# A graph layer on one core: edges sorted tile by tile into three places a bin, instead of three tiles together into nine

## The chip, the cores and the metric

The kernel runs on one core of one Trainium2 chip. The metric is the device time of one execution in microseconds (us), the median of several runs. Of the engines, TensorE (PE) multiplies matrices, VectorE (DVE) and ScalarE (ACT) work elementwise, GpSimd (POOL) issues the indirect transfers here, and SyncE (SP) issues most of the plain ones. All transfers share the core's 16 DMA engines. Matmuls write into PSUM, a small memory of banks with 2 KB per partition; everything else lies in SBUF (128 partitions) or in DRAM.

## The reference

A graph has 6250 nodes with 64 features and 206250 directed edges with 64 features. Each edge takes the features of one of its nodes (`col`), makes a 128-wide hidden vector, and adds its result to its other node (`row`):

```python
msg = concatenate([x[col], edge_attr], axis=1)       # 128 wide
h = relu(msg @ W1a.T + b1a)                          # 128 wide, per edge
h = h @ W1b.T + b1b
sums = segment_sum(h, row, num_segments=n_nodes)
agg = sums / maximum(counts, 1.0)[:, None]
z = relu(concatenate([x, agg], axis=1) @ W2a.T + b2a) @ W2b.T + b2b
out = concatenate([z, x], axis=1) @ Wr.T + br
y = layernorm(x + out)
```

The edges come sorted by `dst`, which is the node whose features are gathered; the node that receives the sum (`src`) is in no order. Bringing each edge's hidden vector to the node that it is added to is what most of the kernel does. The second matrix of the edge network is linear, so the kernel applies it after the sum, per node.

## The kernel before

**Tiles, blocks, bins.** The edges are padded to 1612 tiles of 128, grouped in 124 blocks of 13 tiles. The receiving nodes are grouped in 49 bins of 128. An edge's row is 130 numbers (`W`): its 128 hidden values, a one for the count, and the number of its node inside its bin. The goal is to have, for each bin, tiles of 128 rows that all belong to the bin; then a one-hot matrix of the node numbers (`nodes_of`, L1504, on DVE) and one matmul per tile (`summed`, L1524) add them to the bin's 128 sums. Matmuls in plain f32 run as two instructions each; the profile counts these.

**Two ways for a row.** Tiles of a block go one of two ways.

- *Direct*: the first layer is computed per tile (`hidden`, matmul L1372, ReLU L1376 on ACT into the ring `orow` of 4 blocks), and GpSimd scatters the 128 rows of the tile with one indirect transfer (`scatter`, L1396) to rows of DRAM (`rows`) that belong to their bins. The place of an edge in its bin is its rank, counted over all blocks by a running count on DVE (`carried`, `bins_of`, the scan L1065) and two bf16 matmuls (`counts_of`, L1104 and L1105); `slots` turns it into the row number `rowidx`.
- *Joined* (blocks 4 to 109, six of the 13 tiles, as two joins of three): the inputs of the edges, not their rows, are sorted on TensorE. A join has 441 fixed places (49 bins of nine, `SLOTS`) and 64 spare places. `join_ranks` and `join_places` give each of the join's 384 edges the next of the nine places of its bin; those that come too late go to the spare places, numbered by `join_past` and `join_at_slots`. `marks` makes a one-hot matrix of 128 x 512 for each tile: two of three on DVE (L1222), the third on ACT in two steps (L1227, L1228). `join` multiplies edge features (`side` and, for the low part, `rest`) with the marks; the three tiles add up in one PSUM bank, with a one-pass f32 type and 512 columns (L1256). ACT copies the result to `rj`. `join_rows`, one step later, computes the first layer from `rj` in chunks of 126 or 128 columns (L1273, L1280, L1281), and `join_store` writes the fixed places with SP to `fixed` in DRAM. Since each join has the same places, no indirect transfer is needed for these. The spare places (`overs`) are scattered by GpSimd as one tile, four blocks later, together with that block's direct tiles.

Empty places are rows of zeros, which cost a sum like others: they make tiles for the matmuls of L1524.

**Epochs.** Rows in DRAM can be summed only when they have landed. The scatters are cut in three epochs of 110, 12 and 2 blocks, each with its own `rows`; inside an epoch, the first tiles of a bin can be read as soon as so many blocks are done that they must be full (`FULL`). The rows in `fixed` can be read in stages of three tiles of places each. A plan worked out when the kernel is built (`groups_at`, with `RATES` as the most tiles per step) gives each step its groups of sums; `read` loads them with SP into nine buffers `rt`, `collect` adds the results to `part`.

**Order.** The loop `for k, ep_ in enumerate(epoch_of)` makes one step per block. PE, ACT, DVE and SP work in the order in which the step issues their instructions: counts of block k+1, first layer of block k (in two or four parts), `join_rows` of block k-1, first half of a group of sums, ranks of block k+1, the last part of the first layer, `join` of block k, second half of the sums. The scatters of block k are issued two steps later (`LEAD`). Some wait by hand for progress of the PE in step k+1 (`pace`, `PACED`), so that scatters don't overtake the first layer and leave it without a lead. Blocks 0 to 3 and 110 to 123 have no joined tiles. During the first steps the kernel also loads `x` (`load_x`, L857), makes tables of the nodes' part of the first layer (`y_rows`, L903) and windows of them (`window`, L1342), and clears the DRAM rows (`clear`).

After the last scatter the last epoch is summed, and 17 groups of nodes go through mean, node network and layer norm (`Nodes`, from L1914).

Of the kernel before, what the change touches and what calls it, by code (L numbers as in the profile page):

```python
# [9 lines left out]
F32 = mybir.dt.float32  # L10
# [443 lines left out]
EPOCHS = (110, 12, 2)  # L454
# [3 lines left out]
FULL = ((3, 6, 9, 12), (1,), ())  # L458
# [5 lines left out]
PRE, AHEAD_FROM, EVERY = 9, 10, 2  # L464
RATES = {0: 55, 2: 18, 3: 10}
RING = 8
# [5 lines left out]
JOIN, JOINS, MARKS = 3, 2, 3  # L472
JOIN_FROM, JOIN_TO = 4, 110
SLOTS, PARTS, WHOLE = 9, 3, 42
RUN = SLOTS // PARTS
SPARE = 64
OVER = 4
OVERS = 7
SORTED = 512
PACED = range(PRE, 123)  # L480
SIDES, ENATS, CHUNK = 2, 2, 2
ON_ACT = 1
# [11 lines left out]
def fast_path(  # L494
# [69 lines left out]
    def joined(k):  # L564
        if not JOIN_FROM <= k < JOIN_TO:
            return 0
        return JOINS
# [4 lines left out]
    def over(k):  # L572

        return int(k >= OVER and joined(k - OVER) > 0)
# [4 lines left out]
    def past_slots(nodes):  # L579

        mean = JOIN * P * nodes * (1 / N - 1 / E)
# [13 lines left out]
    def edges_of(b, n, first=0):  # L595
# [4 lines left out]
        joins = sum(joined(k - OVER) for k in blks if over(k))  # L600
# [3 lines left out]
        return nodes, mean + joins * more, SPREAD * (mean + joins * spread) ** 0.5  # L604
# [50 lines left out]
    GROUPS = -(-NJOIN * PARTS // P)  # L655
    for i in range(GROUPS):
        at = next(k for k in range(JOIN_TO + 1) if join_at[k] * PARTS >= min(P * (i + 1), NJOIN * PARTS))
        hi_ = by_bin((i + 1) * RUN, (i + 1) * RUN)
# [5 lines left out]
    PADT = 4  # L664
# [3 lines left out]
    for e, ep_ in enumerate(epochs):  # L668
        ep_.trash = P * sum(over(k) for k in range(ep_.first, ep_.end))
        ep_.rows = dram.tile([ep_.trash + NB * ep_.stride, W], F32, name=f"rows{e}")  # L670
    ALL = -(-GROUPS * P // (PARTS * JOINS)) * JOINS
    fixed.rows = [dram.tile([ALL * n, W], F32, name=f"fixed{n}") for n in (MAIN, MID)]
# [38 lines left out]
    mvs = const.tile([P, MV, W + 1], F32, name="mv")  # L711
# [33 lines left out]
    def bins(c0, c1):  # L745
# [4 lines left out]
        nc.vector.tensor_copy(hi[:, blks, :BLK], of)  # L750
# [5 lines left out]
    nc.vector.tensor_copy(mvs[:, :, H:], ident[:, None, WIDE : WIDE + 3].to_broadcast([P, MV, 3]))  # L756
    nc.vector.tensor_tensor(mvs[:, :, W], mvs[:, :, W], mvs[:, :, H], op=ALU.add)
# [6 lines left out]
    with (  # L764
# [32 lines left out]
        sorts = [op.tile([P, JOINS * RUN + 1, W], F32, name=f"sorted{i}") for i in range(2)]  # L797
        overs = [op.tile([P, W + 1], F32, name=f"over{i}") for i in range(OVERS)]

# [15 lines left out]
        def join_top():  # L815
            t = Top("join")
            t.marks = [t.tile([P, JOIN, SORTED], F32R, f"marks{i}") for i in range(MARKS)]
            t.sides = [t.tile([P, JT, P], F32R, f"side{i}") for i in range(SIDES)]
            t.rests = [t.tile([P, JT, D], F32R, f"rest{i}") for i in range(SIDES)]
            t.enats = [t.tile([P, JT, D], F32, f"enat{i}") for i in range(ENATS)]  # L820
            t.rjs = [t.tile([P, JOINS * (FIXED + SPARE)], F32, f"rj{i}") for i in range(2)]
# [3 lines left out]
            for side in t.sides:  # L825
                nc.gpsimd.memset(side[:, :, WIDE].bitcast(F32), 1.0)
                nc.gpsimd.memset(side[:, :, WIDE + 1 :].bitcast(F32), 0.0)
            return t
# [106 lines left out]
        def starts_at(tiles):  # L935
# [11 lines left out]
        one_w = const.tile([P, P], BF16, name="one_w")  # L947
        nc.vector.memset(one_w, 1.0)
# [13 lines left out]
        z_ps, near_f, bins_w = (  # L962
            steady[:, RAMP + 2 + HALF * T + a :][:, :n] for a, n in ((0, JT), (JT, NEAR), (JT + NEAR, HALF))
        )
        assert RAMP + 2 + HALF * T + JT + NEAR + HALF <= BANK
        NQB = 2 * HALF
        assert NB == NQB - 1
        bin_ramp = bins_w.bitcast(BF16)
        bins_b = lent(2 * NT + NG * P * 3 // 2 + NEAR * WIN + 3 * P + P // 2, HALF)
        nc.vector.tensor_copy(bins_b.bitcast(BF16), ramp_b[:, :NQB])  # L970
        nc.vector.memset(bins_b.bitcast(BF16)[:, NB:], -1.0)
        nc.vector.tensor_copy(bins_w, bins_b)
# [8 lines left out]

        codes = [const.tile([P, SORTED], F32, name=f"codes{i}") for i in range(JOINS)]

        def join_consts():


            for i, c in enumerate(codes):
                mid, main, past_ = c[:, :MID], c[:, MID : FIXED], c[:, FIXED : FIXED + SPARE]
                if i > 0:
                    past_, main, mid = c[:, :SPARE], c[:, SPARE : SPARE + MAIN], c[:, SPARE + MAIN : FIXED + SPARE]  # L990
                nc.vector.memset(c[:, FIXED + SPARE :], -1.0)
                main = main.rearrange("p (r a b) -> p a r b", a=PARTS, r=RUN)
# [1103 lines left out]
```

## Time and profile before

| What | Before |
|---|---|
| median of 3 runs | 1470.9 us (1469.45 to 1473.61) |
| profiled execution | 1471.28 us |
| its span, first to last instruction | 1469.1 us |
| mean granted TensorE clock | 0.972 |
| busy: PE, DVE, ACT, POOL | 1360.7, 1258.5, 1068.0, 1079.8 us |
| DMA | 380.88 MB, mean 259 GB/s |
| scatters (L1396) | 976 direct, 106 late |
| sum matmuls (L1524) | 3962, two a tile |

The page's slices are 40 equal parts of the span, about 36.7 us each; a digit is the busy share in tenths. In a group's row, the number behind x counts instructions, then come busy us and the mean ns of one; behind the second bar stands the idle time of the engine ahead of these instructions, with what ended it. In a timeline a row is: start, duration, engine, line, operation, and in brackets the idle time before it and its releaser. The duration of a matmul holds its way through the array, so that matmuls overlap; their cost in a row of many is read from start to start. "issue" names idle time in which the profile shows nothing that the engine waited for.

### The profile page before, as it was taken

How to read it: one execution, taken by the hardware profiler on the slowest of the kernel's cores; microseconds unless marked ns; L12 is line 12 of the kernel's file. 1: busy time of each engine (PE TensorE's matmuls, PEld its weight loads, DVE VectorE, ACT ScalarE, POOL GpSimd, SP SyncE). 2: the span in 40 equal slices, each digit the busy share in tenths (PEclk: the TensorE clock that was granted, in tenths of full speed). 3: DMA queues.
4: the chain of work that ended last, by engine and by line, in shares of the span. 5: the costliest groups of instructions: out<-in, count | busy, mean ns of one | idle time of the engine just before them, and what ended most of it. 6: DMA issues, size and time to landing. Idle time of an engine off the chain costs nothing.

```text
span 1469.1 us, 32367 instructions
## 1 busy us (share of the span) xinstructions
PE 1360.7 (93%) x10258; PEld 1201.3 (82%) x10258; DVE 1258.5 (86%) x2704; ACT 1068.0 (73%) x2309; POOL 1079.8 (74%) x1163
## 2 busy tenths in 40 slices
PE   5688888879999999999999999999999989999796
PEld 5566666668888888888889888888888889998685
DVE  8588777788888988999999999999999788797686
ACT  3389988888888888888988989898888743331014
POOL 5777777777777777777777777777777777777733
PEclk9699999999999999999999999999999999999898
DMA  8878977899999999999998978888888899998773
GB/s 204 247 227 271 271 241 236 252 286 262 297 269 294 284 288 277 269 259 271 268 262 253 266 229 247 244 252 251 234 255 257 260 307 336 294 314 257 246 237 95
DMA packets 264910, 380.88 MB, mean 259 GB/s; under 512 B 45418, under 2 KB 202146, under 8 KB 264730
## 3 DMA queue, kind: packets, MB, share of 16 engines
q1 hardware_dynamic: 196521, 270.41, 64.3%
q0 software_dynamic: 34624, 72.09, 15.4%
q10 hardware_dynamic: 33584, 36.22, 8.3%
q8 instruction: 84, 1.38, 0.4%
q14 instruction: 97, 0.79, 0.2%
HBM read 215.06 MB, written 163.48 MB: 258 GB/s over the span
## 4 chain that ended last, share of the span: by engine, by line
PE 65%; DMA 12%; ACT 7%; DVE 7%; issue 5%; POOL 3%; ACTq 1%; SPq 0%; DVEq 0%; POOLq 0%
PE h_ps L1524 26%; PE h_ps L1256 14%; PE h_ps L1372 10%; DMA rows<-orow,rowidx 10%; PE h_ps L1273 6%; POOL rows L1396 2%; ACT orow L1376 1%; PE cnt_ps L1104 1%; PE cnt_ps L1105 1%; PE h_ps L1281 1%; PE h_ps L1280 1%; DMA rows<-over,rowidx 1%; ACT rhs L1327 1%; DVE had L1065 1%; ACT rhs L1329 1%
## 5 line engine op out<-in xcount | busy, mean ns | idle before, releaser
L1396 POOL DMA_INDIRECT rows<-orow,rowidx x976 | 951.9, 975 | 308.1 <-issue 158.9
L1524 PE MATMUL h_ps<-rt,oh 128*128 128x129 f32 x3962 | 484.5, 277 | 14.3 <-DVE oh L1504 10.8
L1524 PEld LDWEIGHTS h_ps<-rt,oh 128*128 128x128 f32 x3962 | 470.6, 193 | 24.3 <-DVE oh L1504 13.7
L1504 DVE TENSOR_TENSOR oh<-ramp,rt 128x768 f32<-128x768 bf16 (+3 forms) x409 | 312.1, 797 | 42.1 <-DMA rt<-rows 31.5
L1372 PE MATMUL h_ps<-mv,rhs 124*128 124x128 f32 x1952 | 276.4, 286 | 28.9 <-ACT orow L1376 28.9
L1372 PEld LDWEIGHTS h_ps<-mv,rhs 124*128 124x128 f32 x1952 | 256.7, 198 | 42.8 <-ACT orow L1376 31.5
L1256 PE MATMUL h_ps<-marks,side 128*128 128x512 f32 x636 | 266.0, 428 | 8.8 <-ACT orow L1376 8.3
L1222 DVE TENSOR_TENSOR marks<-codes,ramp 128x1024 fp32r<-128x1024 f32 x212 | 253.5, 1214 | 0.0
L1256 PE MATMUL h_ps<-marks,rest 128*64 128x512 f32 x636 | 218.3, 397 | 0.0
L1376 ACT ACTIVATE orow<-h_ps 128x384 f32<-128x384 f32 (+1 forms) x284 | 150.7, 536 | 57.1 <-PE h_ps L1372 49.2
L1065 DVE TENSOR_TENSOR_SCAN had<-ramp,bins 128x450 bf16<-128x450 bf16 (+3 forms) x124 | 145.1, 1170 | 28.6 <-ACT bins L1086 13.6
L1273 PE MATMUL h_ps<-mv,rj 128*126 128x130 f32 x1272 | 160.7, 275 | 7.9 <-ACT rj L1261 7.9
L1256 PEld LDWEIGHTS h_ps<-marks,side 128*128 128x128 f32 x636 | 121.7, 191 | 52.9 <-ACT orow L1376 10.7
L1273 PEld LDWEIGHTS h_ps<-mv,rj 128*126 128x126 f32 x1272 | 149.6, 188 | 10.5 <-ACT rj L1261 10.2
L1228 ACT ACTIVATE marks<-marks,ones 128x512 fp32r<-128x512 f32 x212 | 153.1, 722 | 6.9
L1227 ACT ACTIVATE marks<-codes,z_act 128x512 fp32r<-128x512 f32 x212 | 155.3, 732 | 0.0
L1327 ACT ACTIVATE rhs<-rhs,from_win 60x896 f32<-60x896 bf16 (+1 forms) x116 | 129.5, 1117 | 2.8
L1329 ACT ACTIVATE rhs<-rhs,ones 60x896 f32<-60x896 f32 (+1 forms) x116 | 129.3, 1115 | 2.9
L1396 POOL DMA_INDIRECT rows<-over,rowidx x106 | 103.3, 974 | 32.3 <-issue 11.0
L1256 PEld LDWEIGHTS h_ps<-marks,rest 128*64 128x64 f32 x636 | 87.5, 138 | 31.6 <-ACT marks L1228 2.3
L1363 ACT CAST orow<-lohi 128x7 f32<-128x7 bf16 (+1 forms) x124 | 24.3, 196 | 116.0 <-DMA rows<-orow,rowidx 99.4
L1263 ACT COPY rj<-h_ps 128x442 f32<-128x442 f32 x106 | 56.5, 533 | 65.0 <-PE h_ps L1256 65.0
(182 smaller groups left out, 1692.5 us busy)
## 6 DMA issues: line engine op xcount, KB each, us to landing
rt<-fixed SPq DMA_DIRECT2D x112, 390.0 KB
fixed<-sorted SPq DMA_DIRECT2D x106, 383.9 KB
rt<-rows SPq DMA_DIRECT2D x102, 390.0 KB
rt<-rows SPq DMA_DIRECT2D x121, 260.0 KB
rhs<-in_edgeT SPq DMA_DIRECT2D x106, 224.0 KB
enat<-in_edgeJ SPq DMA_DIRECT2D x106, 192.0 KB
rows<-orow,rowidx POOLq DMA_INDIRECT x976
rows<-padrow ACTq DMA_DIRECT2D x12, 1040.0 KB
```

What stands on the lines that cost most here:

```text
L1065: nc.vector.tensor_tensor_scan(had, on[:, : 2 * HALF * t], oh, 0.0, op0=ALU.mult, op1=ALU.add)
L1222: nc.vector.tensor_tensor(m[:, :n, :], codes[i][:, None, :].to_broadcast([P, n, SORTED]), z[:, :n, None].to_broadcast([P, n, SORTED]), op= ...
L1227: nc.scalar.activation(m[:, t, :], codes[i], AF.Square, bias=z_acts[k][:, i * JOIN + t : i * JOIN + t + 1], scale=-1.0)
L1228: nc.scalar.activation(m[:, t, :], m[:, t, :], AF.Relu, bias=ones[:, :1], scale=-1.0)
L1256: done[k, f"turn{i}"] = nc.tensor.matmul(ps[: w.shape[1], :], w, m[:, t, :], start=t + p == 0, stop=last and p == 1).ins.name
L1273: done[k, "join"] = nc.tensor.matmul(ps[:q, j * W : (j + 1) * W], rj[:, c0 + j * q : c0 + (j + 1) * q], m[:, :W], start=True, stop=True).i ...
L1327: nc.scalar.activation(of_win, rel, AF.Square, bias=from_win[D:WIDE, :])
L1372: done[k, c] = nc.tensor.matmul(ps[:, j, :], rhs[:WIDE, of * P : (of + 1) * P], m[:WIDE, :H], start=True, stop=True).ins.name
L1376: nc.scalar.activation(orow_of(k, k0, n)[:, :, :H], ps[:, :n, :], AF.Relu)
L1396: s = nc.gpsimd.indirect_dma_start(out=ep_.rows, out_offset=bass.IndirectOffsetOnAxis(ap=rowidx[:, k % RING * COLS + j :][:, :1], axis=0), ...
L1504: nc.vector.tensor_tensor(res[:, at_tile : at_tile + nb * n, :], ramp[:, None, :].to_broadcast([P, nb * n, P]), node[:, :, None].to_broadc ...
L1524: m = nc.tensor.matmul(of_bin(b), oh[:, at, :], rows, start=i == 0, stop=i == len(of) - 1)
```

## The change

**Sorted tile by tile.** A tile has three places in each bin (147) and 42 spare ones: 189, padded to 190. Each of the three tiles of a join is sorted by itself (`sort`): two matmuls 190 columns wide, nothing added across tiles; two tiles share a PSUM bank, and ACT copies each pair with two strided copies. `marks` makes all three tiles of a join in one DVE operation of 570 columns; none is made on ACT. All marks of a block are made at the top of its step. The ranks need one matmul instead of three, and so do the spare ones.

**Six and nine.** Even blocks have two joins (six tiles joined, seven direct), odd blocks three (nine joined, four direct), from block 2 instead of 4. Each join has its own late tile, so the blocks that follow by four scatter two or three. `join_rows` has nine (even) or fourteen (odd) chunks instead of eight. `fixed` gets 147 rows a joined tile, where it got 147 x 3 a join of three: as many per joined tile.

**Order.** `join_past` and `join_at_slots` (the "prefix counts") move from between the joins to behind the second half of the sums. Odd blocks have all of their first layer in the late part. `starts_at` runs each step, since the number of counted tiles alternates between 9 and 7. The later `load_x` move from the middle to the end of step 2, `load_places` and `joined_places` to earlier steps, `nodes_ahead` behind the prefix counts.

**Sizes.** Epochs of 114, 8 and 2 blocks, `FULL` (4, 8, 12) instead of (3, 6, 9, 12), rates of 20 tiles for joined steps, six buffers `overs` instead of seven, one `rj` instead of two. Fixed rows are read in stages of three tiles of places that hold 128 sorted tiles each. Bins are stored plus one, and empty spare places count as bin 0 with rows of their own.

```diff
-EPOCHS = (110, 12, 2)
+EPOCHS = (114, 8, 2)
-FULL = ((3, 6, 9, 12), (1,), ())
+FULL = ((4, 8, 12), (1,), ())
-RATES = {0: 55, 2: 18, 3: 10}
-RING = 8
+RATES = {0: 55, 2: 20, 3: 20}
+RING = 7
-JOIN_FROM, JOIN_TO = 4, 110
-SLOTS, PARTS, WHOLE = 9, 3, 42
-SPARE = 64
+JOIN_FROM, JOIN_TO = 2, 110
+SLOTS, WHOLE = 3, 42
+SPARE = 42
-OVERS = 7
+OVERS = 6
...
     def joined(k):
         if not JOIN_FROM <= k < JOIN_TO:
             return 0
-        return JOINS
+        return 2 + k % 2
...
     def over(k):
-        return int(k >= OVER and joined(k - OVER) > 0)
+        return joined(k - OVER) if k >= OVER else 0
...
         def marks(k, i):
-            m = top.marks[(join_at[k] + i) % MARKS]
-            z = z_ps[:, i * JOIN : (i + 1) * JOIN]
-            n = JOIN - ON_ACT
+            t = slice(i * JOIN, (i + 1) * JOIN)
             nc.vector.tensor_tensor(
-                m[:, :n, :], codes[i][:, None, :].to_broadcast([P, n, SORTED]),
-                z[:, :n, None].to_broadcast([P, n, SORTED]), op=ALU.is_equal,
-            )
-            for t in range(n, JOIN):
-                nc.scalar.activation(m[:, t, :], codes[i], AF.Square, bias=z_acts[k][...], scale=-1.0)
-                nc.scalar.activation(m[:, t, :], m[:, t, :], AF.Relu, bias=ones[:, :1], scale=-1.0)
+                top.marks[(join_at[k] + i) % MARKS], codes[:, None, :].to_broadcast([P, JOIN, PITCH]),
+                z_ps[:, t, None].to_broadcast([P, JOIN, PITCH]), op=ALU.is_equal,
+            )
...
+        def sort(k, t0):
+            n = min(2, JOIN * joined(k) - t0)
+            ps = hp.tile([P, BANK], F32, name="h_ps")
+            for i in range(n):
+                of, m = ps[:, i * PITCH : (i + 1) * PITCH], mark_of(k, t0 + i)
+                nc.tensor.matmul(of, top.sides[k % SIDES][:, t0 + i, :], m, start=True, stop=False)
+                done[k, "turn"] = nc.tensor.matmul(
+                    of, top.rests[k % SIDES][:, t0 + i, :], m, start=False, stop=True
+                ).ins.name
+            rj, v = top.rjs[0], ps[:, : n * PITCH].rearrange("p (t c) -> p t c", c=PITCH)
+            nc.scalar.copy(rj[...], v[:, :, : MAIN + SPARE]...)
+            nc.scalar.copy(rj[...], v[:, :, MAIN + SPARE : SORTED])
...
-            pace = {6: 9, 8: BLK - 1, 10: "turn1", 12: "rest"} if j0 else {}
+            pace = {
+                2: {6: 9, 8: BLK - 1, 10: "turn", 12: "rest"}, 3: {9: BLK - 1, 11: "turn", 13: "rest"}
+            }.get(joined(k), {})
...
-            *parts, last_part = {0: ((0, 4), (4, 3), (7, 3), (10, 3)), 2: ((6, 4), (10, 3))}[joined(k)]
+            *parts, last_part = {0: ((0, 4), (4, 3), (7, 3), (10, 3)), 2: ((6, 4), (10, 3)), 3: ((9, 4),)}[joined(k)]
...
-            for i in range(joined(k)):
-                join(k, i)
-                if after and i == 0:
-                    join_past(k + 1)
+            for t in range(0, JOIN * joined(k), 2):
+                sort(k, t)
...
             if g and joined(k):
                 sum_rest(k, g)
                 issue(k)
+            if after:
+                join_past(k + 1)
+                join_at_slots(k + 1)
```

More of the change, by code (lines that the diff above doesn't have):

```diff
@@ L599, in edges_of @@
         tiles = sum(direct(k) for k in blks)
-        joins = sum(joined(k - OVER) for k in blks if over(k))
+        sorted_ = JOIN * sum(over(k) for k in blks)
         nodes = min(N, (b + 1) * P) - b * P
@@ L669, in fast_path @@
         ep_.trash = P * sum(over(k) for k in range(ep_.first, ep_.end))
+        ep_.empty = P * sum(over(k) for k in range(ep_.first, min(AGAIN, ep_.end)))
+        assert max(ep_.empty, ep_.trash - ep_.empty) <= P * 255 or ep_.first > 0
         ep_.rows = dram.tile([ep_.trash + NB * ep_.stride, W], F32, name=f"rows{e}")
-    ALL = -(-GROUPS * P // (PARTS * JOINS)) * JOINS
-    fixed.rows = [dram.tile([ALL * n, W], F32, name=f"fixed{n}") for n in (MAIN, MID)]
+    fixed.rows = [dram.tile([GROUPS * P * n, W], F32, name=f"fixed{n}") for n in (MAIN, MID)]
     relt = dram.tile([NGR, NG * P], BF16, name="relt")
@@ L1243, in side @@
             else:
[L1244 to L1264 removed]
+                nc.vector.tensor_tensor(top.rests[k % SIDES][:, :n, :D], e[:, :n, :], s[:, :n, :D], op=ALU.subtract)
@@ L1266, in join_rows, with mids, part @@
+        def mids(k):
+            n = JOIN * joined(k) * MID
+            return [(0, 0)] + [(n - Q, 2 * Q - n)] * (n > Q)
         def join_rows(k):
             _, _, m = made[k]
-            rj, rows, q = top.rjs[k % 2], sorts[k % 2], P - 2
-            mains = (JOINS * MID, JOINS * MID + MAIN + JOINS * SPARE)
-            for i, c0 in enumerate(mains):
+            rj, rows, g = top.rjs[0], sorts[k % 2], joined(k)
+            def part(r, i):
+                c0 = (r * JT + i * JOIN) * WHOLE
+                return rj[:, c0 : c0 + Q]
+            for i in range(g):
@@ L1271, in join_rows @@
                 ps = hp.tile([P, BANK], F32, name="h_ps")
[L1272 to L1275 removed]
+                for r in range(SLOTS):
+                    nc.tensor.matmul(ps[:Q, r * W : (r + 1) * W], part(r, i), m[:, :W], start=True, stop=True)
                 nc.scalar.activation(
[L1277 removed]
+                    rows[:Q, i * SLOTS : (i + 1) * SLOTS, :], ps[:Q, : SLOTS * W].rearrange("p (j f) -> p j f", f=W), AF.Relu
@@ new lines, in join_rows @@
+            for i in range(g):
+                nc.tensor.matmul(of[:, i], part(SLOTS, i), m, start=True, stop=True)
+            nc.scalar.activation(overs[k % OVERS][:Q, :g, :], of, AF.Relu)
+            ps = hp.tile([P, BANK], F32, name="h_ps")
+            n = len(mids(k))
+            of = ps[:Q, : n * W].rearrange("p (j f) -> p j f", f=W)
+            for i, (c0, _) in enumerate(mids(k)):
+                done[k, "join"] = nc.tensor.matmul(
+                    of[:, i], rj[:, JT * (MAIN + SPARE) + c0 :][:, :Q], m[:, :W], start=True, stop=True
+                ).ins.name
@@ L1740, in fast_path @@
             if joined(k):
-                marks(k, 0)
+                for i in range(joined(k)):
+                    marks(k, i)
                 collect(0)
@@ L1764, in fast_path @@
                 g = sum_first(k) if due > 0 else None
-            for i in range(1, joined(k)):
-                marks(k, i)
             if after:
```

274 lines of the change are left out of this document (115 added, 159 removed).

## The prediction

> **What bounds the kernel now.** I read the page's busy lines and slices first, then the scatters' line by source, GpSimd's timeline, the windows, and last the chain of the final 140 us. The page makes TensorE look like the bound:
>
> ```profile
> span 1469.1 us, 32367 instructions
> PE 1360.7 (93%) x10258; PEld 1201.3 (82%) x10258; DVE 1258.5 (86%) x2704; ACT 1068.0 (73%) x2309; POOL 1079.8 (74%) x1163
> POOL 5777777777777777777777777777777777777733
> L1396 POOL DMA_INDIRECT rows<-orow,rowidx x976: 962/967/1523, 14.1 to 1399.2; - x196
> L1396 POOL DMA_INDIRECT rows<-over,rowidx x106: 963/968/1186, 113.1 to 1233.8; - x106
> 14.11 1.15 POOL L1396 DMA_INDIRECT rows<-orow,rowidx  x1 [9.54 <-ACT orow L1376]
> ...
> 499.14 0.96 POOL L1396 DMA_INDIRECT rows<-orow,rowidx  x1 [0.30 <-issue]
> 500.41 0.97 POOL L1396 DMA_INDIRECT rows<-orow,rowidx  x1 [0.30 <-issue]
> ...
> 529.68 0.97 POOL L1396 DMA_INDIRECT rows<-orow,rowidx  x1 [0.30 <-ACT side L1237]
> ```
>
> But GpSimd's slices are flat, and its timeline says why. From the scatter at 499.14 to the one at 529.68 lie 24 intervals: 30.54 / 24 = 1.2725 us each, 0.97 busy and 0.30 between, whatever is named as the releaser. There are 976 + 106 = 1082 scatters; from the first start (14.1) to the last (1399.2) pass 1385.1 us, and 1081 x 1.2725 is 1375.6. Only 9.5 us are lost anywhere. The scatter queue runs back to back for 94% of the span, and a busy share of 74% is as full as it gets. The other engines sit closely below it:
>
> ```profile
> 50.00:70.00 20.00, 14.15 (x63) 11.68 (x63) 11.05 (x21) 4.06 (x10) 15.43 (x16) 0.50 0.91 261
> 100.00:300.00 200.00, 168.86 (x1091) 131.89 (x1090) 153.59 (x356) 182.55 (x397) 152.13 (x158) 0.96 0.85 257
> 300.00:500.00 200.00, 194.20 (x1467) 170.43 (x1466) 177.47 (x369) 175.20 (x380) 152.12 (x156) 1.00 0.99 280
> 900.00:1100.00 200.00, 199.63 (x1543) 176.91 (x1542) 187.71 (x390) 174.98 (x375) 152.13 (x157) 1.00 0.85 247
> 1280.00:1300.00 20.00, 20.00 (x180) 19.83 (x180) 17.59 (x40) 6.05 (x8) 15.12 (x17) 1.00 1.03 347
> ```
>
> (Columns: stretch, its length, busy us of PE, PEld, DVE, ACT, POOL, then granted clock, DMA share, GB/s.) GpSimd's 152.1 per 200 us is the same in each. PE is full late, DVE at 94%, the DMA engines full from 300 to 500.
>
> **The change, part by part.** The steady price is in scatters, so I count them. Before, a joined block has 7 direct and 1 late one: 8. After, an even block has 7 + 2 and an odd one 4 + 3: 16 a pair, as before, 16 x 1.2725 = 20.36 us. *Nothing in the steady cadence moves.* What does fall is the start: blocks 2 and 3 now join too. Direct scatters: 54 x 7 + 54 x 4 + 16 x 13 = 802; late ones 54 x 2 + 54 x 3 = 270; together 1072, ten fewer. **Term 1: 10 x 1.2725 = -12.7 us.**
>
> *The start.* Blocks 0 and 1 occupy the queue to 14.1 + 26 x 1.2725 = 47.2. Blocks 2 to 5 then gave 13 + 13 + 7 + 7 = 40 scatters (50.9 us); now 7 + 4 + 7 + 4 = 22 (28.0 us). The queue asks for block 4 at 47.2 + 11 x 1.2725 = 61.2, block 5 at 70.1, block 8 (after 27 more) at 95.6. ACT wrote those rows before at:
>
> ```profile
> 52.46 0.65 PE L1342 MATMUL h_ps<-w1x_t,rt 65*60 65x128 f32 x2 [5.01 <-DMA rt<-in_xT]
> 55.17 0.49 ACT L1376 ACTIVATE orow<-h_ps 128x384 f32<-128x384 f32 x1 [1.52 <-PE h_ps L1372]
> ...
> 73.75 0.49 ACT L1376 ACTIVATE orow<-h_ps 128x384 f32<-128x384 f32 x1
> 84.62 0.49 ACT L1376 ACTIVATE orow<-h_ps 128x384 f32<-128x384 f32 x1
> ...
> 113.49 0.49 ACT L1376 ACTIVATE orow<-h_ps 128x384 f32<-128x384 f32 x1
> ```
>
> These are the last rows of blocks 3, 4, 5 and 8. At that pace the queue would run dry by 74.2 - 61.2 = 13 us at block 4, and 114.0 - 95.6 = 18 at block 8. Against that: ACT loses its marks, and the x loads (L857) go behind a later step, where the 5.01 us of the first row were lost to a window load behind them. So the cost lies between 0 and 18. The 5.01 and, over the four steps to block 8, some 1.6 us of ACT each (next part) come off it: 18 - 5 - 6 = 7, and the new memsets of GpSimd lie in its 9.54 idle before the first scatter at no cost (without that cover, below 3 us by the 0.5 us that such fills take). I take 5, since a scatter starts with its block's first rows, not its last. **Term 2: +5 us.**
>
> *The steady blocks.* Durations of before:
>
> ```profile
> L1222 DVE TENSOR_TENSOR marks<-codes,ramp 128x1024 fp32r<-128x1024 f32 x212 | 253.5, 1214 | 0.0
> L1227 ACT ACTIVATE marks<-codes,z_act 128x512 fp32r<-128x512 f32 x212 | 155.3, 732 | 0.0
> L1228 ACT ACTIVATE marks<-marks,ones 128x512 fp32r<-128x512 f32 x212 | 153.1, 722 | 6.9
> L1261 ACT COPY rj<-h_ps 128x505 f32<-128x505 f32 x106 | 61.0, 575 | 6.5 <-PE h_ps L1256 6.5
> L1504 DVE TENSOR_TENSOR oh<-ramp,rt 128x768 f32<-128x768 bf16 x214 | 196.4, 952 | 24.3 <-DMA rt<-rows 14.9 <-DMA rt<-fixed 6.5
> L939 DVE MEMSET ramp<- 128x375 f32 x5 | 1.9, 371 | 0.6 <-DVE marks L1222 0.3 <-DVE rhs L1334 0.2
> 649.09 1.50 PE L1524 MATMUL h_ps<-rt,oh 128*128 128x129 f32 x12
> 650.43 0.35 PE L1104 MATMUL cnt_ps<-had,less_ones 128*128 128x450 bf16 x1
> ...
> 651.70 1.50 PE L1273 MATMUL h_ps<-mv,rj 128*126 128x130 f32 x12
> 653.03 0.38 PE L1280 MATMUL h_ps<-mv,rj 128*126 128x130 f32 x2
> ...
> 656.04 0.39 PE L1256 MATMUL h_ps<-marks,rest 128*64 128x512 f32 x1
> 656.27 0.40 PE L1256 MATMUL h_ps<-marks,side 128*128 128x512 f32 x1
> ```
>
> By start to start: the 12 sum matmuls take 1.34 us, 0.112 each, two a tile; a chunk matmul of `join_rows` 1.33 / 12 = 0.111, two a chunk; a 512-wide sort matmul 0.23. Per pair of blocks, on PE: sort 24 x 0.23 = 5.5 becomes 30 narrow ones. No row has a 190-wide one of that type; the bounds are 0.112 (as narrow as the f32 ones, limited alike by their weights) and 0.23 (no gain at all from a third of the width). I take 0.112, as the f32 rows are nearest in width: 3.4. `join_rows` 16 chunks become 23: 3.6 to 5.1. Direct tiles 14 become 11: 3.1 to 2.5. With counts and ranks PE drops from about 14.0 to 12.2 us a pair without sums. DVE: four marks of 1.214 become five of 0.74 (570 of 1024 elements, with the fixed part), two refills of 0.46 for the alternating counts come on top, the rest stays: 14.0 both times (187.7 us in 19.65 steps, less sums of 13.5 tiles). ACT: four marks of 1.454 go, eight pairs of copies, about 0.6 a pair (the 505-wide copy took 0.575), replace six copies: -3.2 us a pair. None of this is on the path while the scatters are: **price 0**, covered by 20.36 us a pair.
>
> The sums are what moves. Fixed rows come as 147 a tile, read three or four tiles a bin, and the plan has 2162 tiles for 1981, 538 reads for 409, and none before step 40, where sums ran from step 29. Steps 40 to 57 then carry 20 tiles each, where before they had 14. PE there: 12.2 + 40 x 0.2234 = 21.1 us a pair; DVE: 14.0 + 40 x 0.167 (0.952 / 6 and the adds) = 20.7. Both pass 20.36. DMA: 280 GB/s x 10.18 us = 2.85 MB a block; six more tiles (66.6 KB each) and the stores (+0.1 MB) make 3.35, which takes 12.0 us at 280 GB/s, 9.7 at the 347 of the window from 1280. Over 17 blocks that is 0 to 30 us, late for PE through `rt`, next for `orow`. Four row buffers let the first layer run up to two blocks, 20 us, ahead of the queue, which swallows most of it. The pacing of even blocks on `done[k + 1, 9]`, now a late part of the odd step, costs nothing while that lead stands. **Term 3: +3 us (0 to 30).**
>
> *The end.*
>
> ```profile
> 1366.10 2.43 DMA rows<-orow,rowidx
> 1368.68 3.71 DMA rt<-rows
> 1372.48 0.97 DVE oh L1504
> 1373.49 13.40 PE h_ps L1524 x100
> ...
> 1400.16 16.78 issue
> 1416.95 0.84 POOL agg L1927
> 1360.00:1380.00 20.00, 10.04 (x64) 9.29 (x64) 9.08 (x18) 0.00 (x0) 15.22 (x16) 0.74 0.59 194
> ```
>
> After the last scatter 16.8 us pass before the first node group. A landing, a read, a one-hot and one sum would be 2.4 + 3.7 + 1.0 + 0.7 = 7.8, so 9 at most can be won; PE's backlog of epoch 1, 170 tiles read from 1368.7 on, makes the difference, and it shrinks to 106 tiles with the epoch of 8. But the plan puts 1058 sum tiles behind step 110 where there were 849: 209 x 0.2234 = 47 us more, against idle time such as the 10 us of the last row. If PE can't place them it ends up to 10 us later. **Term 4: -2 us (-9 to +10).**
>
> Sum: 1469.1 - 12.7 + 5 + 3 - 2 = 1462.4. The profiled execution took 1471.3, 2.2 more than its span, and lies at the median of 1470.9, so the forecast is 1464.6, **1465**.
>
> **Rule and row.** For the narrow sort the Trainium skill, "TensorE: Matmul & The Clock Gate", section "Back-to-back issue gap", says an isolated matmul is spaced by its moving width over 2.4 GHz and a little: an estimate of 82 ns for 190, so by it the weights would decide and the 0.112 stand; 512 gives 216, and this trace has 230. It doesn't speak of this type at small widths. By it the sum would be the same, and a rate that falls with width is the rival D below.
>
> **Rivals.** B, *the start is covered*: rows of block 4 come by 61 and terms 2 and 3 vanish: with term 4 at -4, 1469.1 - 12.7 - 4 + 2.2 = **1455**. For it: ACT idles in 50:70 (4.06 of 20 busy). Against: PE ran there at a granted 0.50. C, *the sums starve the queue* in steps 40 to 57 and again from 57 to 74: DMA's 30 us less what the lead covers, 25 net with the second stretch, and the scatters then follow PE step by step through `done[k + 1, 9]`: 1465 + 25 = **1490**. It decides from 10.2 us a block on DMA, PE or DVE. For it: share 0.99 already from 300 to 500. Against: no scatter was late in that stretch. D, *the narrow matmul is no faster than the wide*: 30 x 0.23 = 6.9 instead of 3.4, so PE takes 12.2 + 3.5 + 8.9 = 24.6 us a pair in steps 40 to 57, 4.2 over the queue (9 pairs, 38 us), 3 over it to step 74 (25 us), about 17 at the end of it all less a lead of 20: some **1525**; at the f32 rate per column (0.2234 / 129 x 190 = 0.33) beyond 1580. E, *the clock*: steps 2 to 40 carry no sums, PE has 12.2 of 20.36 us to do and waits in one piece; at the 0.50 granted in 50:70 it needs 24.4, 4 us over per pair, 19 pairs: 1465 + 68 less the lead, at worst **1513**. Against: 100:300 had few sums, 169 of 200 busy, and 0.96. The Trainium skill, same page, Part 1, has the clock halve after an idle window of about 3.4 us; by that rule a wait in one piece brings E about, and the granted 0.50 behind the 5.01 us wait agrees with it. F, *no effect*: PE and ACT work goes, the bound stays, start and sums eat ten scatters: that is the upper half of my own case.
>
> **How the numbers follow.** A, the sum with its bounds (1455 to 1478), 0.44: faster 0.21, no change 0.17, slower 0.06. B 0.22, faster. C 0.20, of it 0.02 no change. D 0.09, E 0.05, slower. A measurement here tells 0.3% (4.4 us; the runs shown lie 4.2 apart) from no change. Together: faster 0.43, same 0.19, slower 0.38. The range runs from 1448 (B with the full 7.8 end) to 1500 (C with 35 instead of 25); most of D and E lies beyond.
>
> **What would show it.** Term 1: 802 + 270 scatters, still 1.27 apart in 500:530. Term 2: gaps of GpSimd between 55 and 100 us. Term 3: gaps between 430 and 600, each released by PE or `rt`. Term 4: the `issue` piece ahead of the first `agg`. D: start to start of the sort matmuls near 0.11 or near 0.23. E: granted clock from 100 to 430. If GpSimd's intervals exceed 1.27 in the steady blocks themselves, the view of a fixed queue is wrong and so is the sum.

## The result

The changed kernel takes 1603.7 us (median of 3, 1602.16 to 1607.58) where the kernel before takes 1470.9: a ratio of 1.0905, 95% interval 1.0866 to 1.0944. The forecast was 1465, the range ended at 1500. On some chips the kernel before itself takes 1826 to 1859 us, with gaps between the scatters in all blocks of every kernel that was profiled there; runs that fell there are set only against each other and are marked "late chips" below.

The profile page of the changed kernel, its busy lines and two of its slices:

```profile
span 1601.9 us, 35079 instructions
PE 1373.4 (86%) x10984; PEld 1312.1 (82%) x10984; DVE 1310.4 (82%) x2926; ACT 909.3 (57%) x2573; POOL 1078.6 (67%) x1155
POOL 6667666654377777666777777777777777777513
DMA  7888768788998999999999998888889999999984
```

GpSimd's slices are no longer flat: a dip from the fifth slice on, deepest in the eleventh, and a shallow stretch behind it. ACT lost 159 us of work, and DVE and PE did about what they did before: no engine became the bound of the whole. The scatters by source, and the windows (columns as in the prediction):

```profile
L1393 POOL DMA_INDIRECT rows<-orow,rowidx x802: 962/967/1537, 15.6 to 1510.8; - x161
L1393 POOL DMA_INDIRECT rows<-over,rowidx x270: 962/967/1471, 86.9 to 1345.5; - x135
...
100.00:300.00 200.00, 148.38 (x991) 139.00 (x991) 125.33 (x295) 122.22 (x357) 132.49 (x137) 0.85 0.79 214
300.00:500.00 200.00, 129.41 (x910) 120.68 (x908) 131.48 (x307) 115.47 (x338) 114.99 (x118) 0.81 0.85 211
500.00:700.00 200.00, 183.86 (x1502) 179.29 (x1503) 166.23 (x365) 135.00 (x395) 143.36 (x146) 0.95 0.99 280
700.00:900.00 200.00, 189.94 (x1631) 183.47 (x1630) 188.84 (x396) 136.67 (x395) 142.53 (x146) 1.00 0.99 274
900.00:1100.00 200.00, 181.44 (x1535) 173.94 (x1534) 188.36 (x433) 145.13 (x420) 152.97 (x155) 1.00 0.89 249
```

802 + 270 = 1072 scatters came, as counted. GpSimd's busy time fell from 152.1 to 115.0 in one stretch, with PE, DVE and ACT all idle for a third of the time or more beside it, and the DMA share at 0.85: nothing was full there, things waited for each other. Only from 900 on is the queue full again.

To place the loss I took, for each block, the time from its first scatter to that of the next block, less 1.2725 us a scatter: the gaps of the queue. With the wait between the end of the last scatter and the first node group (us; the three kernels on the right are explained below):

| Blocks | Before | Changed | g1: nodes | e5: + zeroing early, sums evened | h2: the same, zeroing late |
|---|---|---|---|---|---|
| 0 to 8 | 1.0 | 15.5 | 18.2 | 18.9 | 17.8 |
| 8 to 30 | 0.8 | 41.2 | 2.5 | 24.6 | 2.9 |
| 30 to 36 | 1.5 | 35.2 | 27.1 | 1.8 | 0.4 |
| 36 to 50 | 0.7 | 1.9 | 2.4 | 14.9 | 14.9 |
| 50 to 74 | 3.4 | 28.3 | 30.3 | 3.3 | 1.8 |
| 74 to 110 | 2.1 | 7.7 | 7.7 | 6.8 | 20.0 |
| 110 to the end | -0.3 | 2.1 | -0.6 | 0.0 | 0.0 |
| wait after the last scatter | 16.8 | 38.8 | 39.1 | 35.6 | 34.6 |
| span | 1469.1 | 1601.9 | 1557.8 | 1536.6 | 1523.1 |
| time of one run | 1471.3 | 1603.7 | 1559.7 | 1538.4 | 1525.0 |

The spans differ by 132.8 us: the first scatter starts 1.5 later, ten scatters fewer are -12.7, the gaps are 122.8 more (132.0 less 9.2), the wait 22.0 more, the node groups 0.8 less. Nothing is left over.

### The profile page after: what moved, and what is told of

Same layout as the page of the kernel before. It is cut to its first block, busy times and chain, and to the rows that moved or that the text cites. A ratio compares the mean times of both kernels' runs of the same rounds, so it can differ in the third digit from the quotient of the medians.

```text
span 1601.9 us, 35079 instructions
## 1 busy us (share of the span) xinstructions
PE 1373.4 (86%) x10984; PEld 1312.1 (82%) x10984; DVE 1310.4 (82%) x2926; ACT 909.3 (57%) x2573; POOL 1078.6 (67%) x1155
## 4 chain that ended last, share of the span: by engine, by line
PE 45%; DVE 18%; DMA 17%; issue 9%; ACT 5%; POOL 3%; ACTq 1%; SPq 1%; DVEq 0%; POOLq 0%
PE h_ps L1520 22%; PE h_ps L1367 7%; DMA rows<-orow,rowidx 6%; PE h_ps L1259 5%; DVE marks L1199 4%; DMA rows<-over,rowidx 4%; POOL rows L1393 3%; DVE oh L1500 3%; ACT rj L1235 3%; DMA xrs<-nx 2%; PE h_ps L1266 2%; DVE side L1213 1%; DMA fixed<-sorted 1%; PE h_ps L1230 1%; PE h_ps L1231 1%
## 5 line engine op out<-in xcount | busy, mean ns | idle before, releaser
L1393 POOL DMA_INDIRECT rows<-orow,rowidx x802 | 785.8, 980 | 350.0 <-issue 132.5
L1520 PE MATMUL h_ps<-rt,oh 128*128 128x129 f32 x4324 | 532.6, 279 | 52.6 <-ACT rj L1239 29.9
L1500 DVE TENSOR_TENSOR oh<-ramp,rt 128x384 f32<-128x384 bf16 (+3 forms) x538 | 348.8, 685 | 33.4 <-DMA rt<-fixed 19.4
L1393 POOL DMA_INDIRECT rows<-over,rowidx x270 | 265.3, 982 | 103.1 <-issue 54.6
L1259 PEld LDWEIGHTS h_ps<-mv,rj 128*126 128x126 f32 x1620 | 207.4, 201 | 43.1 <-ACT rj L1235 36.7
L1230 PE MATMUL h_ps<-marks,side 128*128 128x190 f32 x810 | 202.1, 290 | 29.9 <-ACT orow L1371 26.9
L1231 PE MATMUL h_ps<-marks,rest 128*128 128x190 f32 x810 | 193.0, 280 | 0.0
L1199 DVE TENSOR_TENSOR marks<-codes,ramp 128x570 fp32r<-128x570 f32 x270 | 186.7, 741 | 1.1
L1235 ACT COPY rj<-h_ps 128x336 f32<-128x336 f32 (+1 forms) x432 | 182.5, 447 | 2.7 <-PE h_ps L1231 1.8
L1057 DVE TENSOR_TENSOR_SCAN had<-ramp,bins 128x500 bf16<-128x500 bf16 (+3 forms) x124 | 144.0, 1162 | 21.8 <-ACT orow L1358 9.6
L1231 PEld LDWEIGHTS h_ps<-marks,rest 128*128 128x128 f32 x810 | 159.6, 197 | 0.0
L1266 PE MATMUL h_ps<-mv,rj 128*126 128x132 f32 x540 | 86.0, 293 | 38.6 <-DVE nx L1691 36.7
L1266 PEld LDWEIGHTS h_ps<-mv,rj 128*126 128x126 f32 x540 | 73.9, 201 | 42.4 <-DVE nx L1691 38.5
```

The costliest lines, as they stand in the source:

```text
L1057: nc.vector.tensor_tensor_scan(had, on[:, : 2 * HALF * t], oh, 0.0, op0=ALU.mult, op1=ALU.add)
L1199: nc.vector.tensor_tensor(top.marks[(join_at[k] + i) % MARKS], codes[:, None, :].to_broadcast([P, JOIN, PITCH]), z_ps[:, t, None].to_broad ...
L1230: nc.tensor.matmul(of, top.sides[k % SIDES][:, t0 + i, :], m, start=True, stop=False)
L1231: done[k, "turn"] = nc.tensor.matmul(of, top.rests[k % SIDES][:, t0 + i, :], m, start=False, stop=True).ins.name
L1235: nc.scalar.copy(rj[:, : JT * (MAIN + SPARE)].rearrange("p (r t b) -> p t r b", t=JT, b=WHOLE)[:, t0 : t0 + n], v[:, :, : MAIN + SPARE].re ...
L1259: nc.tensor.matmul(ps[:Q, r * W : (r + 1) * W], part(r, i), m[:, :W], start=True, stop=True)
```

## The experiments

### The node work in each step

The changed kernel's waits of VectorE from 90 to 400 us (total, times, longest), and its timeline in one step (start, length, engine, and in brackets the idle time before it with its releaser):

```profile
DVE nx L1691 <- DMA xrs<-nx: 64.6, 8, 8.8
...
227.74 0.56 DVE L1691 COPY nx<-h_ps 128x384 f32<-128x384 f32 x1 [7.59 <-DMA xrs<-nx]
228.22 1.40 DVE L1199 TENSOR_TENSOR marks<-codes,ramp 128x570 fp32r<-128x570 f32 x2
228.35 0.94 PE L1266 MATMUL h_ps<-mv,rj 128*126 128x132 f32 x6 [2.91 <-DVE nx L1691]
229.71 0.43 SPq L1696 DMA_DIRECT2D xrs<-nx  x1
```

`AHEAD_FROM, EVERY = 8, 1` makes a chunk of node work in each of the steps 8 to 32, 25 chunks; before, it was `10, 2`. The excerpt under "The change" doesn't show this line. There is one buffer `nx`; its store to `xrs` is issued in the next step, and `nodes_ahead` at the end of that step waits until it has landed. VectorE works in order, so the marks of the next step stand behind that wait, and PE's `join_rows` (L1266) waits for the same copy, by its own row. Undone alone (runs e1, f1 and g1 are one kernel; the first two fell on late chips). The edit also halves the node work per step, so it is the list of waits that speaks for the store:

```diff
-PRE, AHEAD_FROM, EVERY = 9, 8, 1
+PRE, AHEAD_FROM, EVERY = 9, 10, 2
```

> The changed kernel, with the node work spread as before: nodes_ahead in every second step from step 10 (AHEAD_FROM, EVERY = 10, 2) instead of in each from step 8. Theory: in the changed kernel the store of one chunk (xrs<-nx) lands 8 to 9 us after its issue and the next nodes_ahead waits for it on VectorE within the same step, so steps 8 to 32 run in a loop of latencies; the gaps of the scatter queue between 130 and 380 us, 42 us together, fall below 12 and the kernel takes 1603.7 - 35 = 1569 us (1558 to 1580). Rival: the queue starves there because of the shorter ring of late rows (six) or the halved clock without sums; then the gaps stay and the time is within 8 us of 1604.

> The kernel of e1 again (node work in every second step from 10), beside a kernel before that is back at 1470 us. As there: the gaps of blocks 8 to 30 (41 us) fall below 12 and the time to 1569 us (1558 to 1580) if the loop through the chunk's store makes them; within 8 us of 1604 if the six rings of late rows or the clock do.

> The kernel of e1 (only the node work spread as before), once more. Beside a kernel before near 1470: the 41 us of gaps of blocks 8 to 30 fall below 12 and the time to 1569 us (1558 to 1580) if the store of a node chunk, for which VectorE waits 70 us in the changed kernel, makes them; if the clears that ScalarE issues make them (e5 still had 25 us there), only to 1580 to 1600.

g1 took 1559.7 us beside 1472.2 of the kernel before: 44 less than the changed kernel, and the gaps of blocks 8 to 30 went from 41.2 to 2.5. Its waits in the same stretch, and a window:

```profile
DVE nx L1691 <- PE h_ps L1687: 6.7, 11, 0.7
...
200.00:300.00 100.00, 78.25 (x560) 73.48 (x560) 76.39 (x174) 71.89 (x211) 76.49 (x78) 0.85 0.88 245
```

The wait for `xrs` is no longer in the list. The window also tells on the clock: 0.85 granted, and yet the queue is full (76.49 in 100 us); the changed kernel has 0.83 in the same stretch and GpSimd at 61.91. So the low clock of the changed kernel was a companion of the waiting there, not its cause. On late chips the edit can't be read: ratios 1.0825 (1.0645 to 1.1005) and 1.0848 (1.0709 to 1.0987) against 1.0832 for one run of the changed kernel, with 41.6 and 51.2 us of gaps in blocks 12 to 30 against its 48.3.

The same two constants put into the kernel before. To stand as in the changed kernel, `nodes_ahead` (with `nodes_load`) also moves behind the prefix counts, so this is one edit more than g1 undoes:

```diff
-PRE, AHEAD_FROM, EVERY = 9, 10, 2
+PRE, AHEAD_FROM, EVERY = 9, 8, 1
...
-            if k in nodes_at:
-                nodes_ahead(nodes_at[k])
...
             if after:
                 join_at_slots(k + 1)
...
+            if k in nodes_at:
+                nodes_ahead(nodes_at[k])
```

> The kernel before, with only the node work changed as in the changed kernel: nodes_ahead in each step from 8 on, and behind join_at_slots. Theory: the loop through the store of the chunk is this edit's own, so the old kernel loses 20 to 45 us too: 1490 to 1516. Rival: it costs only where the queue has no lead to spare, as in the changed kernel, and the old one stays within 5 us of 1471.

> The kernel before with the node work in each step from 8 on and behind join_at_slots, and nothing else changed (the kernel of e4 again; beside a kernel before of 1829 us it cost 1.1%). Theory: the wait for the chunk's store is this edit's own, so where the kernel before takes 1470 us this one loses about what the changed kernel won when the edit was undone (44 us): 1495 to 1515, with gaps in blocks 8 to 32. Rival: the old kernel's steps have a longer lead, so that the wait is covered: 1470 to 1478.

k1 took 1491.6 us beside 1468.6: 23 us, half of what it costs in the changed kernel and just short of the range. Its gaps lie in blocks 26 to 36 (18.4 us), not from block 8 on. The old kernel comes to step 8 with 1.0 us of gaps where the changed one has 15.5, so it may still have a lead to spend; that wasn't tried. VectorE's two longest waits here, from 90 to 400 us:

```profile
DVE nx L1698 <- PE h_ps L1694: 35.0, 15, 3.7
DVE nx L1698 <- DMA xrs<-nx: 21.4, 6, 5.0
```

The first is the wait for the chunk's own matmuls, so how much of the 23 us is the store's isn't shown. On a late chip the edit cost 1.1% (e4; 1.0059 to 1.0157). So it costs by itself, and about twice as much in the changed kernel.

### The zeroing of the unused fixed places

The fixed places are read in seven stages of 128 sorted tiles, 896 in all, of which 810 exist. `clear_rest` writes zeros to the other 86 in step 30. The transfers of it in the changed kernel and, in the second fence, in the kernel before:

```profile
fixed<-padrow ACTq DMA_DIRECT2D x1, 5502.7 KB
fixed<-padrow ACTq DMA_DIRECT2D x1, 917.1 KB
```

```profile
fixed<-padrow ACTq DMA_DIRECT2D x1, 383.9 KB
fixed<-padrow ACTq DMA_DIRECT2D x1, 64.0 KB
```

6.6 MB instead of 0.46. In the changed kernel's timeline of ScalarE and GpSimd the last work of ScalarE ends at 381.9; the second transfer's issue starts at 398.18 and occupies its queue for 15.73 us, and the queue of scatters runs dry for 27.76:

```profile
379.82 0.35 ACTq L1437 DMA_DIRECT2D fixed<-padrow  x1
380.89 1.04 ACT L1322 ACTIVATE rhs<-rhs,from_win 60x896 f32<-60x896 bf16 x1
398.18 15.73 ACTq L1437 DMA_DIRECT2D fixed<-padrow  x1
413.95 0.49 ACT L1371 ACTIVATE orow<-h_ps 128x384 f32<-128x384 f32 x1 [32.02 <-issue]
414.72 0.96 POOL L1393 DMA_INDIRECT rows<-orow,rowidx  x1 [27.76 <-ACT orow L1371]
```

By the chain of waits, what landed last before the issue at 398.18 was a store of sorted rows that took 12.10 us. SyncE's queue waited 28.9 us for a transfer of the zeros, and in g1, where the gap at step 30 stays (second fence), ScalarE's wait is put down to one as well:

```profile
386.06 12.10 DMA fixed<-sorted
398.18 15.73 ACTq L1437
...
SPq L855 <- DMA fixed<-padrow: 29.1, 2, 28.9
```

```profile
ACT orow L1371 <- DMA fixed<-padrow: 38.5, 1, 38.5
```

The zeroing cut in twelve pieces, first alone (e2, f2), then together with the node edit (e3, f3 and e3_again), with the changed kernel as the base of these late chips (after_again):

```diff
-        def clear_rest():
+        def clear_rest(i):
+            t0, t1 = (NSORT + (GROUPS * P - NSORT) * j // CLEAR for j in (i, i + 1))
...
-            if k == EARLY:
-                clear_rest()
+            if k in range(6, 6 + 2 * CLEAR, 2):
+                clear_rest((k - 6) // 2)
```

> The changed kernel, with the zeroing of the unused places of the fixed rows (86 tiles of 147 rows, 6.6 MB) cut in twelve pieces in the even steps 6 to 28 instead of two transfers in step 30. Theory: ScalarE's queue stands for 16 us behind the second transfer and the first keeps the other transfers waiting; the scatter queue's one gap of 28 us at 387 us goes, and the kernel takes 1603.7 - 30 = 1574 us (1565 to 1582). Rival: the cost is the 6.6 MB themselves (23 us at 285 GB/s), which then slow steps 6 to 28 instead; the time stays above 1592.

> The kernel of e2 again (zeroing in twelve pieces). The gap of 31 us in blocks 30 to 32 goes and the time is 1574 us (1565 to 1582); above 1592 if the bytes cost the same elsewhere.

> Both edits of the last two runs together. If the two losses are separate they add: 1603.7 - 35 - 30 = 1539 us (1528 to 1550). If they share one cause (a lead that is lost once and then missing), the sum is smaller: 1560 or more. Theory for what is left: the first 100 us (15 us of gaps), steps 40 to 74 (27 us of gaps between 600 and 800 us) and 39 us instead of 17 between the last scatter and the first node group.

> The kernel of e3_both once more, since the kernel before took 1829 us beside it instead of 1471, with all transfers late. With the kernel before near 1471, the two losses add to 1603.7 - 35 - 30 = 1539 us (1528 to 1550); with one shared cause 1560 or more; gaps of the scatter queue between 130 and 440 us below 15 us instead of 76.

> The kernel of e3 again. From e5, which has the evened sums on top and took 1538: if the evened sums are worth 20, this one takes 1555 to 1562, and the two losses of f1 and f2 add less than fully; if they add fully (1539), the evening is worth nothing in time, and what it saved in blocks 50 to 74 was lost elsewhere.

> The changed kernel as it is, as the base for the runs that were taken while the kernel before needed 1829 us. If the chip is back to the kernel before near 1471, this takes 1600 to 1608 us. If not, every transfer is late for both kernels; with the separate losses of the nodes' loop and the zeroing on top it takes 1829 x 1.09 = 1994 us (1975 to 2010); if late transfers hide these losses, as little as 1960.

All of these fell on late chips: e2 1961.8 and f2 1984.5 us (ratios to the kernel before 1.0697, 1.0564 to 1.0830, and 1.0699, 1.0609 to 1.0788), e3 1954.6 and f3 1995.3 (1.0658, 1.0525 to 1.0791, and 1.0757, 1.0698 to 1.0816), e3_again 1959.3, the changed kernel 2008.1 beside 1853.8, inside the 1975 to 2010 expected for such a chip. The times expected beside 1470 can't be tested on them. The one gap can be read even there: blocks 30 to 32 have 29.9 us in the changed kernel, 36 to 37 with the node edit alone, and 2.4 to 4.4 with the pieces. Whether the bytes cost elsewhere can't be read there. That took e5 (below; pieces in steps 6 to 28) and the same kernel with the pieces in steps 78 to 100 (h1 on a late chip, h2):

> e5 (node work in every second step, zeroing in pieces, sums evened) with the twelve pieces of the zeroing in steps 78 to 100 instead of 6 to 28. g1, without pieces there, has 2.5 us of gaps in blocks 8 to 30 where e5 has 25, and ScalarE waits 54 us for clears in e5. Theory: the pieces and the clears of the scattered rows together fill ScalarE's queue; moved, the gaps of blocks 8 to 30 fall to under 6 and those of 36 to 50 (16 us) stay or fall, and beside a kernel before near 1470 it takes 1510 us (1500 to 1520): 1602 - 44 (nodes) - 27 (zeroing) - 25 (sums) - 2. What is left to 1470 is the start (18 us of gaps against 13 saved) and 19 us of TensorE's backlog at the end. Rival: 6.6 MB cost the same wherever they are written; then blocks 74 to 104 take over 15 us of gaps and the time stays at 1530 to 1540.

> The kernel of h1 again, for a chip on which the kernel before takes 1470 us: 1510 us (1500 to 1520) if the place of the pieces cost e5 its 25 us in blocks 8 to 30; 1530 to 1540, with over 15 us of gaps in blocks 74 to 104, if the bytes do.

h2 took 1525.0 us beside 1472.4, between the two forecasts: the gaps of blocks 8 to 30 fell from e5's 24.6 to 2.9, but those of 74 to 110, where the pieces now lie, rose from 6.8 to 20.0. (h1, late: 1987.5 beside 1859.3, nothing to read.) So the pieces remove 25 to 27 us at step 30 and cost 22 in the early steps and 13 in the late ones: neither of the two theories holds whole. In the early steps ScalarE's queue pays, in e5 from 90 to 400 us:

```profile
ACT orow L1371 <- DMA rows<-padrow: 53.7, 8, 8.5
```

g1, without pieces there, has 10.1 us of this wait for the clears of the scattered rows, and from 100 to 350 us the DMA engines moved no more in e5 (239 GB/s at a share of 0.91) than in g1 (241 at 0.88). In the late steps of h2 ScalarE waits for no clear, but the DMA share from 843 to 1090 us is 0.99 where e5 has 0.88. There the cost fits the bytes: 6.6 MB are an estimated 23.5 us at the 280 GB/s of the window from 500 to 700. No run parts the bytes from their place fully.

### The sums crowded into steps 40 to 57

e5 is e3 with the sums spread:

```diff
-FULL = ((4, 8, 12), (1,), ())
+FULL = ((3, 6, 9, 12), (1,), ())
-RATES = {0: 55, 2: 20, 3: 20}
+RATES = {0: 55, 2: 15, 3: 15}
...
-            until = min(o for o in opens if o > k)
+            until = k + 1 if joined(k) else min(o for o in opens if o > k)
```

> e3 (both edits) with the sums spread: FULL (3, 6, 9, 12), 15 tiles a joined step at most and no deadline per stage, so that sums begin at step 31 and a joined step never has more than about 15 tiles where e3 has 20 in steps 40 to 57. Theory: in the changed kernel the scatter queue starves in blocks 50 to 74 because PE and VectorE have over 20.36 us a pair of blocks there; beside a kernel before near 1471 the gaps of blocks 50 to 74 fall from 28 us to under 8 and the time by 20 (from about 1539 to 1519), while the 39 us between the last scatter and the first node group stay. Rival: these gaps come from DMA latency or the pacing on the late part of odd steps, and stay. With the kernel before near 1829 instead, all blocks have gaps, and the fall in blocks 50 to 74 (about 70 us in e3) should be under 15 us, as latency decides there.

1538.4 us beside 1470.2, not the 1519 expected; what the evening alone is worth in time isn't known, since e3 has no run beside 1470. The gaps of blocks 50 to 74 fell from 28.3 to 3.3, so the crowding made them. (The pieces of the zeroing, which e5 has too, don't explain it: on late chips these blocks have 105 to 119 us with the pieces, in e3 and f3, and 106 and 116 without, in e1 and f1.) PE's timeline of the changed kernel shows a pair of steps there, and the narrow sort matmuls:

```profile
701.64 0.37 PE L1106 MATMUL cnt_ps<-had,less_ones 128*128 128x450 bf16 x1
...
706.85 0.28 PE L1230 MATMUL h_ps<-marks,side 128*128 128x190 f32 x1
706.97 0.27 PE L1231 MATMUL h_ps<-marks,rest 128*128 128x190 f32 x1
707.08 0.28 PE L1230 MATMUL h_ps<-marks,side 128*128 128x190 f32 x1
...
724.44 0.37 PE L1106 MATMUL cnt_ps<-had,less_ones 128*128 128x450 bf16 x1
```

From 701.64 to 724.44 is one pair: 22.8 us of nearly unbroken PE work, with 88 sum matmuls or 44 tiles (9.8 us), against 20.36 of the queue. From 600 to 880 us no wait of PE is longer than 2.6 us and none is for a transfer, though the DMA share is 0.97 to 1.02: this speaks for PE setting the pace there. What e5 gained there it lost in part: 14.9 us of gaps in blocks 36 to 50 that the changed kernel doesn't have, as many in h2. Their cause wasn't tried.

### TensorE's backlog at the end

The end of the chain of waits of the changed kernel, and the window behind its last scatter (1511.8):

```profile
1465.55 43.82 PE h_ps L1520 x392
1509.52 0.97 POOL rows L1393
1510.80 0.97 POOL rows L1393
1511.77 38.80 issue
1550.57 0.83 POOL agg L1915
...
1500.00:1520.00 20.00, 20.00 (x160) 18.32 (x159) 18.02 (x38) 0.00 (x0) 9.02 (x10) 1.00 1.03 300
1520.00:1540.00 20.00, 19.60 (x169) 18.85 (x168) 20.00 (x38) 0.00 (x0) 0.00 (x0) 1.00 0.90 267
```

PE is nearly full for as long as the node groups wait. To test it I left sums out: from e3 the last two stages of fixed rows (f6), and from e5 the last stage alone (e9). e9 also leaves out the count of missing edges, by which f6 falls back on its general path; the edges that are left out are missing from its output:

```diff
+        summing.pop()
         summing += [(st,) for st in steps[len(epochs[0].full) : -1]]
```

> e3 without the sums of the last two stages of fixed rows (294 tiles, which the plan opens at step 113; the output lacks them): 66 us less TensorE work after step 110. Theory: the wait of 39 us between the last scatter and the first node group is TensorE's backlog, so it falls to 17 us or below (8 at the least) and the time by 20 to 30 us against f3. Rival: the wait is the landing and reading of the last rows; then it stays above 30 us.

> e5 without the sums of the last stage of fixed rows (147 tiles, opened at step 113; the output lacks them and the test of the edge count is made to pass): 147 x 0.2234 = 33 us less TensorE work behind step 110. Theory: the 36 us between the last scatter and the first node group are TensorE's backlog, so with a kernel before near 1470 they fall to 8 to 17 us and the time from 1538 to 1510 to 1520. Rival: they are the landing and reading of the last rows, and stay above 30 us. With the kernel before near 1830 the wait falls from about 70 us by 20 to 40 likewise.

f6 says nothing, since it took that path as well: 7786 us. e9 ran on the late chip of f3. The wait, as the chain of each kernel has it, first f3, then e9:

```profile
1870.73 70.00 issue
1940.73 0.84 POOL agg L1916
```

```profile
1858.63 42.46 issue
1901.09 0.84 POOL agg L1917
```

33 us less TensorE work shorten the wait by 27.5, inside the 20 to 40 expected for a late chip. That e9 has evened sums and f3 not makes no difference here: h1, with them, waited 71.8 on another late chip. So there the wait is to a large part the backlog; beside 1470 it wasn't tried, and the full PE is what speaks for it.

### The start

In the changed kernel the queue of scatters stood twice in the first 90 us:

```profile
70.48 0.96 POOL L1393 DMA_INDIRECT rows<-orow,rowidx  x1 [7.58 <-ACT orow L1371]
...
86.93 0.97 POOL L1393 DMA_INDIRECT rows<-over,rowidx  x1 [6.58 <-DVE rowidx L1172]
```

The first of these waits is for rows of the first layer, which the prediction priced; the second is for the row numbers of the first late tile, made on VectorE, which it didn't. k2 and k3 are h2 with `JOIN_FROM = 4`; both fell on late chips.

> The kernel of h2 with joined blocks from 4 on instead of 2 (JOIN_FROM = 4), as in the kernel before: 1082 scatters instead of 1072. Theory: ten scatters more cost 12.7 us, and the gaps of blocks 2 to 8 (18 us in h2) fall below 3, so the start gains at most 3 to 5 us by it: 1518 to 1524 beside a kernel before near 1470. Rival: the gaps of the first blocks stay (late loads, slow clock) and the time grows to 1533 to 1540.

> The kernel of k2 again, for a chip on which the kernel before takes 1470 us: 1518 to 1524 us if the run-dry start is made by the early joins (gaps of blocks 2 to 8 below 3 us), 1533 to 1540 if not.

1945.1 us beside 1829.8 and 1966.3 beside 1841.3, where h1 took 1987.5 beside 1859.3. Blocks 2 to 8 still have 24 and 28 us of gaps there (h1: 32). The early joins may be worth about nothing, as the prediction's first two terms would have it, but these runs don't show it: it stays open.

## Why the prediction was wrong

**What bounds it: right.** The queue's 1.27 us a scatter and 1072 scatters held, and all of the loss but the 1.5 us of the later first scatter is a gap of that queue or the wait behind it. What failed is the step from "the queue is the bound" to "none of this is on the path".

**Term 1, -12.7: right.** Ten fewer scatters, same spacing (from 505.69 to 514.60 us seven intervals, 1.273 each).

**Term 2, +5: too small.** Measured 14.5 us of gaps (15.5 less 1.0) and a first scatter 1.5 later, inside the bounds of 0 to 18. The 18 from the pace of before was nearly the answer, and the 13 us that I took off it didn't come. That it comes so near is partly luck: 6.6 us of the gaps are the wait for a late tile's row numbers, which wasn't in the term.

**"The steady blocks: price 0": the step that failed most.** It covered the sort, the marks and the rows, and these held: the narrow sort matmul is spaced 0.11 us, as taken, so rival D was wrong. (By the isolated spacing in the Trainium skill's page "TensorE: Matmul & The Clock Gate", section "Back-to-back issue gap", the width alone would make an estimated 82 ns; the rows show 110. That the weights set the rest is argued, not shown.) But two edits of that stretch had no price at all. The text nowhere costs the node work in each step: 40 us of gaps (blocks 8 to 30). Undoing it took away 39 of them and 8 in blocks 30 to 36, and gave back 44 in time. Its cover would have been one step between the store and the next use of `nx`; that was taken away. And it never follows the larger number of fixed stages to the places that no tile fills: 6.6 MB of zeros in one step, 34 us (blocks 30 to 36).

**Term 3, +3 of 0 to 30: mis-sized.** Blocks 36 to 74 have 26 us more gaps. PE took 22.8 us for a pair instead of 21.1 (44 sum tiles instead of 40, and 13.0 us for the rest instead of 12.2); blocks 40 to 50 have only 0.6 us, as a lead would have it, but no longer. That is rival C, to which I gave 0.20. Its price of 25 is nearly exact by luck, since it was worked out from the DMA engines, and the waits point to PE.

**Term 4, -2 of -9 to +10: wrong sign.** The wait grew by 22. The 47 us of added work behind step 110 stood in the text; that PE would find room for most of it was assumed, and PE was full instead.

**Rival E, the clock: wrong as a cause.** The clock did fall to 0.81 from 300 to 500 us, where PE was busy 129 of 200, but g1 keeps the queue full at 0.85. The Trainium skill's rule on the clock gate ("TensorE: Matmul & The Clock Gate", Part 1: half the clock after an idle window of about 3.4 us) agrees with the fall beside idle PE; it didn't set the time. The rival's own sum is off as well: 19 pairs at 4.04 us are 77, not 68, so with the lead of 20 it would have said 1522, not 1513.

**Together.** The four terms were to make -6.7 us of span. The same four measure -12.7 + 16.0 + 26.1 + 22.0 = 51.4, which alone gives 1523, outside the range. The two edits without a price bring 74.1 more, the blocks from 74 on 8.0, less 0.8 in the node groups. The best version tried (h2, 1525.0) undoes the one, moves the other and evens the sums, and its span is still 54.0 over that of before: gaps of 16.8 at the start, 14.2 in blocks 36 to 50, 17.9 in 74 to 110 and -0.3 elsewhere, 17.8 of wait, 1.5 of later start, less 12.7 for ten scatters and 1.2 in the node groups. So even this version, without the node edit and with the zeros moved, loses more than the ten scatters gain.

## What to carry to other kernels

When a queue is the bound and its feeders run a few per cent below it, list every changed constant and ask of each which single buffer it now uses at what interval, and which transfers follow from it; here the two edits outside the sum cost more than all terms in it. Rows that become readable late make sums that can only be done late: count what is left when the bound resource has finished. And set a gain at the start against the queue that it may run dry: here 12.7 us against 16.0.

## What the runs showed of the hardware

A transfer issue isn't always short on ScalarE: behind a transfer of 5.5 MB the next issue took 15.73 us, where the median issue of its clears takes 0.37, and ScalarE did no work for 32 us around it. The one-pass f32 matmul 190 wide is spaced 0.11 us, half of the 0.23 at 512 wide. GpSimd's scatters of 128 rows kept their 1.27 us in both kernels. A copy into `nx` waited up to 8.8 us for the landing of a 64 KB store issued in the same step, at a mean DMA share of 0.79 from 100 to 300 us.
